# Attention over a graph mask, one core: half of the first mask pieces written as bytes by ScalarE and stored from SyncE, and another way through the last tail

## The chip, the cores and the metric

The kernel runs on one core of a Trainium2 chip. The metric is the device time of one execution in microseconds; lower is better. The median of three runs of the kernel before is 3595.21 us (3592.2 to 3596.22). One execution was profiled; the page and every time below come from it.

In the profile PE is TensorE (PEld its weight loads), DVE is VectorE, ACT is ScalarE, POOL is GpSimd and SP is SyncE. SP computes nothing here: it is the queue from which most plain transfers are issued. POOL issues transfers too, among them all that add to what is already in memory.

## The reference

For each of eight frames there are 2048 rows of 256 channels. One layer is computed, and then a residual and a norm. `adj` is one 2048 x 2048 mask for all frames and heads.

```python
def layer(x, adj, ...):                       # x: (8, 2048, 256), H = 8 heads of D = 32
    q, k, v = split(x @ w_qkv)                # each (F, N, H, D)
    scores = einsum('fnhd,fmhd->fhnm', q, k) / sqrt(D)
    scores = where(adj > 0, scores, -1e9)
    t = einsum('fhnm,fmhd->fnhd', softmax(scores), v)
    x = layernorm(x + t, ln1_g, ln1_b)
    f_out = relu(x @ w1 + b1) @ w2 + b2
    return layernorm(x + f_out, ln2_g, ln2_b)
out = layernorm(x + layer(x, adj, ...))       # the last norm has no scale or shift
```

## The kernel before

**Items.** The attention is cut into 1024 items (f, qc, g, mb): frame, one of four chunks of 512 queries, one of two groups of four heads, one of sixteen blocks of 128 keys. `scores` (L202) makes four 128x512 score tiles on PE; DVE adds the mask to two at a time (L213), which also moves them out of PSUM; ACT takes the exponential of all four (L217); `values` (L221) multiplies by V and adds up in one PSUM bank over the sixteen blocks.

**Sums of the exponentials.** The denominators need the sum over the sixteen blocks. `add_up` (L242) folds the tiles: blocks 0, 3, 6, 8, 11, 13 and 15 by additions on POOL (L249), two chains of four by accumulating transfers from POOL's queue (L246), block 14 stays alone. `denominator` (L273) multiplies the four remaining tiles by a matrix of ones on PE (L283), turns the result (L290) and takes reciprocals on DVE (L295).

**The tail of a chunk.** After the second head group, `outcome` (L302) turns the attention output on PE (L313), multiplies it by the reciprocals on DVE (L314) into `y`, and adds the rows of `x` to it with an accumulating transfer from POOL's queue (L317). `tail` (L321) does norm 1, turns the rows (L330), runs the feed-forward layer (L341, L342, L351), adds it to `y` (L353), does norm 2, multiplies by the scale and adds the shift on POOL (L356, L358), adds `x` once more by an accumulating transfer (L360), does norm 3 and stores 512 KB from SP (L363). `norm` (L252) takes statistics of four 256-channel rows on DVE (L256, L257), makes the reciprocal root for all four in four small POOL operations (L260 to L264, the power on L261), and applies it in four ACT instructions (L267).

**Order.** Every engine executes in the order in which the program emits its instructions; there is no reordering by a scheduler. The loop over items (L457) emits the attention. Everything else is a generator in the list `fill`: `start` (L369) adds one with a time and a due item, and `advance` (L375) moves each on by one `yield`. A `yield` of a number waits so many items; `BANK` asks for the one bank that an item may give away; `ROOM` allows two tails at a time. While items run, `bank` (L85) hands out the one PSUM bank that is not collecting the values (`state["side"]`, L87); in the first stretch, where no side is set, it goes round five. After the last item a loop (L483) moves the generators on until they end. Since the order is that of emission, a tail that is cut by many yields lies scattered behind the work of others, and one with few yields lies together.

**The first stretch.** `begin` (L404) loads the mask as sixteen int32 pieces of 512 x 512 (`fetch`, L408, one MB each, from SP). For each piece, a conversion on DVE makes bf16: 0 where there is an edge, -57344 where not (L426). `mask_blocks` (L117) turns it on PE in two halves of eight 128x128 transposes into a PSUM bank each (L124), and DVE writes each half as fp8 (L127); the result goes to the DRAM tile `MD` through POOL's queue (L128, 128 KB a half), from where later chunks reload it. In the first four pieces `begin` also turns the rows of frame 0 (L430), stores them to the DRAM tile `XD` through POOL's queue (L431), and makes keys and values; in the next four keys and values of the second head group (L437). Two score items are computed after the eighth piece (L443). All of these use tiles of the pool `pp` (11 buffers); a fetch is emitted after the conversion of each piece, five pieces ahead.

Of the kernel before, what the change touches and what calls it, by code (L numbers as in the profile page):

```python
# [11 lines left out]
BF16 = mybir.dt.bfloat16  # L12
I32 = mybir.dt.int32
F8 = mybir.dt.float8e5
AF = mybir.ActivationFunctionType
# [3 lines left out]
P = 128  # L19
# [10 lines left out]

MASKED = -57344.0


# [20 lines left out]
def fast_path(ctx, tc, cst, x, adj, out, RS):  # L54
# [62 lines left out]
    def mask_blocks(qc, mc, cv, to=None):  # L117
        for half in range(2):
            yield BANK
            ps = bank(BF16)  # L120
            for r in range(2):
                for j in range(TPC):
                    rr = 2 * half + r
                    nc.tensor.transpose(ps[:, r, j * P:(j + 1) * P], cv[:, j, rr * P:(rr + 1) * P], identb)  # L124
            k = 2 * mc + half
            m = to[half] if to else mask_piece(0, qc, k)
            nc.vector.tensor_tensor(m, ps, cst["ones"][:, 0:1, None].to_broadcast([P, 2, CH]), ALU.min, saturate=False)  # L127
            nc.gpsimd.dma_start(MD[qc, k], words(m))  # L128

# [108 lines left out]
    MOVED = ((1, 4, 7, 10), (2, 5, 9, 12))  # L238
    ALONE = 14
    SUM = 4  # L240

    def add_up(item):  # L242
        f, qc, g, mb = item
        for chain in MOVED:
            if mb in chain[1:]:
                nc.gpsimd.dma_start(PT[f, qc, g, chain[0]], PT.pop(item), accum_op=ALU.add)  # L246
        if mb in POOLED[1:]:
            first = PT[f, qc, g, POOLED[0]]
            nc.gpsimd.tensor_tensor(first, first, PT.pop(item), ALU.add)  # L249
# [23 lines left out]
    def denominator(f, qc, g):  # L273
        grp = (f, qc, g)
        terms = [PT.pop((f, qc, g, ALONE))] + [PT.pop((f, qc, g, chain[0])) for chain in MOVED + (POOLED,)]
        yield BANK
        ps = bank()
        for n, term in enumerate(terms):
            if n == 2:
                yield BANK  # L280
            for h in range(4):
                r = D * h
                nc.tensor.matmul(ps[r:r + D, :], cst["ones"], term[:, h, :], start=(n == 0), stop=(n == 3))  # L283
        dT = op.tile([P, CH], F32, name="dT")
# [13 lines left out]
        if g == 1:  # L298
            begin = items.index((f, qc, g, LAST)) + SUM + 2
            start(begin, outcome(f, qc), begin)  # L300

    def outcome(f, qc):  # L302
        yield ROOM
        state["tails"] += 1
        rc = RC.pop((f, qc))
        xin = x[f, qc * CH:(qc + 1) * CH, :].rearrange("(p j) c -> p j c", p=P)
        y = yp.tile([P, TPC, C], F32, name="y")
        for gg in range(2):
            oT = OT.pop((f, qc, gg))
            yield BANK  # L310
            ps = bank()
            for j in range(TPC):
                nc.tensor.transpose(ps[:, j * P:(j + 1) * P], oT[:, j::TPC], ident)  # L313
            nc.vector.tensor_tensor(y[:, :, gg * P:(gg + 1) * P].rearrange("p j (h d) -> p j h d", d=D),  # L314
                                    ps.rearrange("p (j h d) -> p j h d", h=4, d=D),
                                    rc[:, :, 4 * gg:4 * gg + 4, None].to_broadcast([P, TPC, 4, D]), ALU.mult)
        nc.gpsimd.dma_start(y, xin, accum_op=ALU.add)  # L317
        begin = items.index((f, qc, 1, LAST)) + SUM + 2
        start(begin + 10, tail(f, qc, y, xin), begin + 26)

    def tail(f, qc, y, xin):  # L321
        yield from norm(y)
        yield TURNED
        state["turned"] = True
# [21 lines left out]
        for jj in range(0, TPC, 2):  # L346
# [6 lines left out]
            nc.vector.tensor_tensor(z[:, jj:jj + 2, :], ps.rearrange("p (b c) -> p b c", c=C), z[:, jj:jj + 2, :], ALU.add)  # L353
        yield 1
        yield from norm(z)
        nc.gpsimd.tensor_tensor(z, z, rows(cst["g2r"]), ALU.mult)  # L356
        yield 1
        nc.gpsimd.tensor_tensor(z, z, rows(cst["be2r"]), ALU.add)  # L358
        yield 1
        nc.gpsimd.dma_start(z, xin, accum_op=ALU.add)  # L360
        yield 7
        yield from norm(z)
        nc.sync.dma_start(out[f, qc * CH:(qc + 1) * CH, :].rearrange("(p j) c -> p j c", p=P), z)  # L363
        state["tails"] -= 1

# [38 lines left out]
    def begin():  # L404
# [16 lines left out]
        while cols:  # L421
# [3 lines left out]
            cv = two[:, c % 2 * TPC * CH:(c % 2 + 1) * TPC * CH].rearrange("p (j m) -> p j m", m=CH)  # L425
            nc.vector.tensor_scalar(cv, col, 0.0, MASKED, op0=ALU.is_le, op1=ALU.mult)  # L426
            fetch()
            xT = rows[c][:, 2:4, :]
            if qc == 0:
                yield from turn_rows(rows[c][:, 0:2, :].rearrange("p a (b c) -> p (a b) c", c=C), xT)  # L430
                nc.gpsimd.dma_start(XD[0][c], xT)  # L431
                XT[0, c] = xT
# [24 lines left out]
    for t, (f, qc, g, mb) in enumerate(items):  # L457
# [4 lines left out]
        if f + 1 < F:  # L462
            for what, *which in NEXT.get((2 * qc + g, mb), []):
                due = t + MB // 2 if what is turn else items.index((f + 1, 0, which[1], which[0] * TPC)) - LEAD - 1
                start(t, what(f + 1, *which), due)
        if mb:
            advance(t, 1)
# [12 lines left out]
        if mb == LAST:  # L480
            start(t + SUM, denominator(f, qc, g), t)
    t = len(items)
    while fill:  # L483
        t += 1
# [237 lines left out]
```

## Time and profile before

| | before |
|---|---|
| median of the runs | 3595.21 us |
| the profiled execution | 3592.91 us |
| its span, first to last instruction | 3590.9 us |
| PE busy | 3199.5 us (89%) |
| DVE busy | 2745.6 us (76%) |
| ACT busy | 2413.7 us (67%) |
| POOL busy | 2628.5 us (73%) |
| mean granted TensorE clock | 0.986 |
| first mask conversion starts | 16.20 us |
| last mask eviction ends | 99.89 us |
| last addition of exponentials on POOL ends | 3524.02 us |
| last activation starts (of four) | 3582.07 us |

In a row of the time line the first number is the start in us from the span's start, the second the duration; then the engine, the line of the kernel, the operation, what it writes and reads with shapes, and how many instructions were merged. In brackets stands how long the engine had been idle before and what ended that. A row of the busy time by stretch gives the stretch, its length, the busy time and instructions of each engine, the granted TensorE clock (1.00 is full), the mean share of the DMA engines and the rate in GB/s.

### The profile page before, as it was taken

The numbers are of one execution on the slowest core, as the hardware profiler recorded it, in microseconds if no ns is written. First come the engines' busy times: TensorE is split into PE (matmuls) and PEld (weight loads), VectorE is DVE, ScalarE is ACT, GpSimd is POOL, SyncE is SP. The second block draws the span as 40 slices with busy tenths as digits, with TensorE's granted clock in tenths as the row PEclk, the third lists the DMA queues.
The fourth block names the chain that finished last, engine by engine and source line by source line (L and its number), as shares of the span: only waits on it lengthen the run. The fifth ranks groups of instructions, "written<-read, shape, count | busy, mean of one in ns | idle before, by whom it ended". The sixth has DMA issues, their size and how long they took to land. (4 is left out here: it accounts for less than half of the span.)

```text
span 3590.9 us, 54434 instructions
## 1 busy us (share of the span) xinstructions
PE 3199.5 (89%) x22020; PEld 1036.2 (29%) x22020; DVE 2745.6 (76%) x3191; ACT 2413.7 (67%) x1921; POOL 2628.5 (73%) x1399
## 2 busy tenths in 40 slices
PE   6889998899988999998989999999998999988884
PEld 4222332223322233222322223222232223322221
DVE  5788768886788867877778776887768877688882
ACT  2576667776677766777677676677667776677772
POOL 3577768787688766878677776787767877688885
PEclk8999999999999999999999999999999999999997
DMA  8677768778578767778667778677776778587763
GB/s 300 138 157 159 171 149 179 153 152 187 130 158 188 154 155 154 155 165 186 156 143 163 158 159 183 131 165 172 156 178 144 151 163 176 137 170 161 152 143 73
DMA packets 146226, 576.52 MB, mean 161 GB/s; under 512 B 14608, under 2 KB 63248, under 8 KB 96816
## 3 DMA queue, kind: packets, MB, share of 16 engines
q0 software_dynamic: 66960, 443.19, 61.0%
q1 hardware_dynamic: 78192, 128.48, 10.5%
q8 instruction: 174, 2.85, 0.3%
q10 hardware_dynamic: 816, 1.31, 0.1%
q14 instruction: 84, 0.69, 0.1%
HBM read 132.52 MB, written 37.75 MB: 47 GB/s over the span
## 5 line engine op out<-in xcount | busy, mean ns | idle before, releaser
L213 DVE TENSOR_TENSOR p<-s,mask 128x1024 f32<-128x1024 f32 x2048 | 2410.2, 1219 | 697.8 <-PE s L210 409.0
L217 ACT ACTIVATE p<-p 128x2048 f32<-128x2048 f32 x1024 | 1957.4, 1911 | 1059.0 <-DVE p L213 820.4
L249 POOL TENSOR_TENSOR p<-p 128x2048 f32<-128x2048 f32 x384 | 1858.4, 4888 | 423.6 <-ACT p L217 421.6
L210 PE MATMUL s<-qT,kT 32*128 32x512 f32 x8192 | 1171.0, 641 | 169.3 <-DVE p L213 165.1
L229 PE MATMUL x<-p,v 128*32 128x512 f32 x8192 | 1092.9, 606 | 0.0
L246 POOL DMA_DIRECT2D p<-p x384 | 385.3, 1022 | 362.3 <-ACT p L217 149.9
L210 PEld LDWEIGHTS s<-qT,kT 32*128 32x128 f32 x8192 | 320.3, 183 | 797.9 <-DVE p L213 648.5
L229 PEld LDWEIGHTS x<-p,v 128*32 128x32 f32 x8192 | 161.3, 108 | 778.5 <-issue 544.1
L267 ACT ACTIVATE y<-y,nb,rs 128x256 f32<-128x256 f32 x384 | 224.9, 589 | 37.8 <-POOL nb L264 37.8
L283 PE MATMUL x<-p,ones 128*32 128x512 f32 x2048 | 243.9, 594 | 2.7 <-POOL p L249 1.2
L167 PE MATMUL x<-in,wqkv 128*128 128x512 f32 x472 | 234.0, 618 | 13.8 <-ACT turned L331 7.8
L256 DVE BATCH_NORM_STATS2 st<-y 128x6 f32<-128x256 f32 x384 | 160.0, 417 | 24.9 <-DMA y<-in_x_dram 24.9
L341 PE MATMUL x<-turned,w1s 128*128 128x512 f32 x256 | 130.6, 633 | 21.3 <-ACT hT L342 20.4
L167 PEld LDWEIGHTS x<-in,wqkv 128*128 128x128 f32 x472 | 79.9, 189 | 174.2 <-issue 71.7
L351 PE MATMUL x<-w2s,hT 128*128 128x256 f32 x512 | 127.6, 392 | 2.6 <-ACT hT L342 1.8
L192 PE MATMUL x<-wqkv,in 128*128 128x128 f32 x896 | 114.9, 281 | 7.2 <-ACT kT L169 7.0
L192 PEld LDWEIGHTS x<-wqkv,in 128*128 128x128 f32 x896 | 104.2, 191 | 55.9 <-ACT kT L169 38.3
L351 PEld LDWEIGHTS x<-w2s,hT 128*128 128x128 f32 x512 | 92.0, 189 | 66.6 <-ACT hT L342 29.4
L283 PEld LDWEIGHTS x<-p,ones 128*32 128x32 f32 x2048 | 63.4, 110 | 163.7 <-issue 124.4
L261 POOL TENSOR_TENSOR rs<-rs,mhalf 128x4 f32<-128x4 f32 x96 | 99.5, 1036 | 8.0
L330 PE MATMUL x<-ident,y 128*128 128x128 f32 x256 | 47.7, 297 | 53.2 <-ACT turned L331 37.7
L358 POOL TENSOR_TENSOR y<-y,be2r 128x1024 f32<-128x1024 f32 x32 | 94.2, 2943 | 0.2
(89 smaller groups left out, 1401.0 us busy)
## 6 DMA issues: line engine op xcount, KB each, us to landing
p<-p POOLq DMA_DIRECT2D x384, 1024.0 KB, 9.8
y<-in_x_dram POOLq DMA_DIRECT2D x64, 512.0 KB, 6.2
mask<-md SPq DMA_DIRECT2D x248, 128.0 KB, 5.7
in<-xd SPq DMA_DIRECT2D x59, 512.0 KB, 7.3
p<-in_adj_dram SPq DMA_DIRECT2D x16, 1024.0 KB, 15.4
out_dram<-y SPq DMA_DIRECT2D x32, 512.0 KB, 4.7
in<-in_x_dram SPq DMA_DIRECT2D x28, 512.0 KB, 5.6
xd<-in SPq DMA_DIRECT2D x28, 512.0 KB, 8.9
```

Source lines behind the costliest of these rows:

```text
L167: nc.tensor.matmul(ps, wqkv[:, a, k0:k0 + P], xT[:, a, :], start=(a == 0), stop=(a == 1))
L192: nc.tensor.matmul(ps[:, j * P:(j + 1) * P], xT[:, a, j * P:(j + 1) * P], wqkv[:, a, 2 * C + g * P:2 * C + (g + 1) * P], start=(a == 0), s ...
L210: nc.tensor.matmul(ps2[half][:, j, :], KT[f, mb // TPC, g][r:r + D, (mb % TPC) * P:(mb % TPC + 1) * P], QT[f, qc, g][r:r + D, :], start=Tr ...
L213: nc.vector.tensor_tensor(pt[:, 2 * half:2 * half + 2, :], ps, MK[f, qc, mb // 2][:, mb % 2, None, :].to_broadcast([P, 2, CH]), ALU.add)
L217: nc.scalar.activation(PT[item], PT[item], AF.Exp, scale=1.0 / math.sqrt(D))
L229: nc.tensor.matmul(O[grp][r:r + D, :], V[f, mb // TPC, g][:, mb % TPC, r:r + D], PT[item][:, h, :], start=(mb == 0), stop=(mb == LAST))
L246: nc.gpsimd.dma_start(PT[f, qc, g, chain[0]], PT.pop(item), accum_op=ALU.add)
L249: nc.gpsimd.tensor_tensor(first, first, PT.pop(item), ALU.add)
L256: nc.vector.bn_stats(st, t[:, j, :])
L267: nc.scalar.activation(t[:, j, :], t[:, j, :], AF.Identity, bias=nb[:, j:j + 1], scale=rs[:, j:j + 1])
L283: nc.tensor.matmul(ps[r:r + D, :], cst["ones"], term[:, h, :], start=(n == 0), stop=(n == 3))
L351: nc.tensor.matmul(ps[:, (j - jj) * C:(j - jj + 1) * C], hT[:, d, j * P:(j + 1) * P], w2s[:, d, :], start=(d == 0), stop=(d == 1))
```

## The change

In the first stretch the conversion is made in two halves by key columns. The first half is written with -5 and the second with -57344 as before. The first half's turned bank is written by ScalarE as signed bytes (the byte of -5 is the bit pattern of -57344 in this fp8 format, and 0 stays 0); the second by VectorE as before. The stores to `MD`, and those of frame 0 to `XD`, go through SP's queue. 

For the last group of the last chunk, blocks 13 and 15 are not added on POOL but become terms of their own in the denominator. The last chunk's tail is a function of its own, `finish`, emitted in one go: the rows of `x` are loaded eight items before the end and added on DVE; the norms work in halves of two rows; scale, shift and residual are four half operations on DVE; the store is in two halves. After the last item, `bank` goes round five banks again. The division (`divide`) and the feed-forward layer (`feed_forward`) become functions that the old and the new tail share.

```diff
 def mask_blocks(qc, mc, cv, to=None):
...
-            nc.vector.tensor_tensor(m, ps, cst["ones"][:, 0:1, None].to_broadcast([P, 2, CH]), ALU.min, saturate=False)
-            nc.gpsimd.dma_start(MD[qc, k], words(m))
+            if half:
+                nc.vector.tensor_tensor(m, ps, cst["ones"][:, 0:1, None].to_broadcast([P, 2, CH]), ALU.min, saturate=False)
+            else:
+                nc.scalar.copy(m.bitcast(I8), ps)
+            nc.sync.dma_start(MD[qc, k], words(m))
...
+    ENDED = (13, 15)
...
-        if mb in POOLED[1:]:
+        if mb in POOLED[1:] and not ((f, qc, g) == items[-1][:3] and mb in ENDED):
...
+        if (f, qc, g) == items[-1][:3]:
+            terms[3:3] = [PT.pop((f, qc, g, b)) for b in ENDED]
...
-            start(begin, outcome(f, qc), begin)
+            start(begin, outcome(f, qc) if (f, qc) != (F - 1, NCK - 1) else finish(f, qc), begin)
...
+    def norm_halves(t):
+        both = []
+        for h in range(0, TPC, 2):
+            mv = small.tile([P, 2, nc.vector.BN_AGGR_DIM], F32, name="mv")
+            for j in range(2):
+                st = small.tile([P, nc.vector.BN_STATS_DIM], F32, name="st")
+                nc.vector.bn_stats(st, t[:, h + j, :])
+                nc.vector.bn_aggr(mv[:, j, :], st)
+            rs = small.tile([P, 2], F32, name="rs")
+            nc.gpsimd.tensor_scalar(rs, mv[:, :, 1], EPS, 1.0, op0=ALU.add, op1=ALU.mult)
+            nc.gpsimd.tensor_tensor(rs, rs, cst["mhalf"][:, 0:2], ALU.pow)
+            nb = small.tile([P, 2], F32, name="nb")
+            nc.vector.scalar_tensor_tensor(nb, mv[:, :, 0], -1.0, rs, op0=ALU.mult, op1=ALU.mult)
+            both.append((h, rs, nb))
+        for h, rs, nb in both:
+            for j in range(2):
+                nc.scalar.activation(t[:, h + j, :], t[:, h + j, :], AF.Identity, bias=nb[:, j:j + 1], scale=rs[:, j:j + 1])
+
+    def finish(f, qc):
+        y = yp.tile([P, TPC, C], F32, name="y")
+        xr, xb = state["rows"], take([P, TPC, C], F32)
+        yield from divide(f, qc, y)
+        nc.vector.tensor_tensor(y, y, xr, ALU.add)
+        norm_halves(y)
+        nc.vector.tensor_tensor(xb, xr, rows(cst["be2r"]), ALU.add)
+        yield from feed_forward(y)
+        z = y
+        norm_halves(z)
+        for h in range(0, TPC, 2):
+            nc.vector.tensor_tensor(z[:, h:h + 2], z[:, h:h + 2], rows(cst["g2r"])[:, h:h + 2], ALU.mult)
+            nc.vector.tensor_tensor(z[:, h:h + 2], z[:, h:h + 2], xb[:, h:h + 2], ALU.add)
+        norm_halves(z)
+        dst = out[f, qc * CH:(qc + 1) * CH, :].rearrange("(p j) c -> p j c", p=P)
+        for h in range(0, TPC, 2):
+            nc.sync.dma_start(dst[:, h:h + 2], z[:, h:h + 2])
...
-            nc.vector.tensor_scalar(cv, col, 0.0, MASKED, op0=ALU.is_le, op1=ALU.mult)
+            for half, what in enumerate((CODE, MASKED)):
+                part = slice(half * 2 * P, (half + 1) * 2 * P)
+                nc.vector.tensor_scalar(cv[:, :, part], col[:, :, part], 0.0, what, op0=ALU.is_le, op1=ALU.mult)
...
-                nc.gpsimd.dma_start(XD[0][c], xT)
+                nc.sync.dma_start(XD[0][c], xT)
...
+        if t == len(items) - MB // 2:
+            state["rows"] = take([P, TPC, C], F32)
+            nc.sync.dma_start(state["rows"], x[f, qc * CH:(qc + 1) * CH, :].rearrange("(p j) c -> p j c", p=P))
...
     t = len(items)
+    state["side"] = None
     while fill:
```

## The prediction

> **What bounds the kernel now.** I read the slices of the page first, then the busy time by stretch, then the time lines of both ends. The change touches only the two ends, so those matter, not the totals.
>
> ```profile
> PEclk8999999999999999999999999999999999999997
> ...
> 62.00:100.00 38.00, 15.17 (x132) 13.07 (x132) 28.85 (x25) 1.91 (x1) 11.04 (x15) 0.50 0.37 136
> 100.00:3500.00 3400.00, 3098.22 (x21376) 972.80 (x21376) 2660.53 (x3076) 2367.32 (x1855) 2549.35 (x1306) 1.00 0.73 159
> 3500.00:3591.00 91.00, 37.85 (x176) 15.72 (x172) 24.07 (x63) 26.27 (x38) 47.17 (x40) 0.72 0.34 75
> ```
>
> The columns of the last three lines are the stretch, its length, the busy time of PE, PEld, DVE, ACT and POOL, PE's granted clock, the DMA share and GB/s. The middle 3400 us run PE at full clock; their instructions and order stay as they were, so I let them shift as a block. From 62 to 100 us no engine is full and PE runs at half clock: this is a chain. ACT has 1.91 us of work there.
>
> *The first stretch* handles 16 adjacency pieces (I call them columns). Columns 8 to 15, from VectorE's time line and then TensorE's:
>
> ```profile
> 62.85 1.22 DVE L426 TENSOR_SCALAR p<-p 128x2048 bf16<-128x2048 int32 x1
> 65.20 1.23 DVE L127 TENSOR_TENSOR in<-s,ones 128x1024 fp8e5<-128x1024 bf16 x1 [1.13 <-PE s L124]
> 66.34 1.22 DVE L127 TENSOR_TENSOR in<-x,ones 128x1024 fp8e5<-128x1024 bf16 x1
> 67.47 1.22 DVE L426 TENSOR_SCALAR p<-p 128x2048 bf16<-128x2048 int32 x1
> ...
> 64.12 1.04 PE L124 MATMUL s<-identb,p 128*128 128x128 bf16 x8 [3.60 <-DVE p L426]
> 64.95 1.06 PE L124 MATMUL x<-identb,p 128*128 128x128 bf16 x8
> ```
>
> One column is 67.47 - 62.85 = 4.62 us: a conversion on DVE, the first eight transposes, then two evictions one behind the other, and PE waits until the next conversion. Columns 0 to 7 are different: PE also makes keys and values there and is busy 4.3 to 5.0 of every 5 us from 10 to 55 us, period 5.8 and then 4.45 us; DVE does not set it.
>
> *The last tail*, from the time line of all engines:
>
> ```profile
> 3524.07 1.06 PE L283 MATMUL x<-p,ones 128*32 128x512 f32 x8 [1.16 <-POOL p L249]
> 3536.37 0.43 DVE L256 BATCH_NORM_STATS2 st<-y 128x6 f32<-128x256 f32 x1 [6.13 <-DMA y<-in_x_dram]
> 3538.97 1.03 POOL L261 TENSOR_TENSOR rs<-rs,mhalf 128x4 f32<-128x4 f32 x1
> 3546.05 3.78 PE L341 MATMUL x<-turned,w1s 128*128 128x512 f32 x4 [0.87 <-ACT turned L331]
> 3550.61 3.78 PE L341 MATMUL x<-turned,w1s 128*128 128x512 f32 x4 [0.78 <-ACT hT L342]
> 3558.04 1.59 PEld L351 LDWEIGHTS x<-w2s,hT 128*128 128x128 f32 x8 [1.28 <-DVE y L353]
> 3567.10 2.34 POOL L356 TENSOR_TENSOR y<-y,g2r 128x1024 f32<-128x1024 f32 x1 [2.19 <-ACT y L267]
> 3569.52 2.34 POOL L358 TENSOR_TENSOR y<-y,be2r 128x1024 f32<-128x1024 f32 x1
> 3577.84 0.43 DVE L256 BATCH_NORM_STATS2 st<-y 128x6 f32<-128x256 f32 x1 [14.87 <-DMA y<-in_x_dram]
> 3582.07 2.07 ACT L267 ACTIVATE y<-y,nb,rs 128x256 f32<-128x256 f32 x4 [15.05 <-POOL nb L264]
> ```
>
> Everything here is one serial chain: two residual loads stand on it (6.1 and, with the two POOL passes, 13 us), and PE waits for its single free PSUM bank. The last activation ends at 3584.14, the span 6.76 later.
>
> **The first stretch, part by part.** The conversion becomes two of 1024 elements; the first half's transposes wait for the first alone. That half is evicted by ACT, the other by DVE.
>
> A half conversion has no row. From one 1.22 us row for 2048 it is 0.61 if all of it scales. The Trainium skill (VectorE: DVE Perf Modes, the section on the TRN2 errata) speaks against this: each VectorE instruction carries a fixed term, about 150 cycles as measured there, or 0.156 us at 0.96 GHz. Then a half is (1.22 - 0.16)/2 + 0.16 = 0.69. The row of 1.22 agrees with 1067 ns of elements plus that term, so I take 0.69; the second half begins 0.09 before the first ends, as evictions do (1.23 long, 1.14 apart), and ends at 1.29. Now one column, at half clock: first transposes start at 0.73, issue for 0.83 (64.95 - 64.12), the second eight follow at 1.56, end at 2.62; DVE evicts from 2.66; the next conversion starts 1.14 later. Period **3.80** (3.72 by plain scaling), against 4.62. Eight columns: 8 x 0.82 = **6.6 us**. ACT's eviction, estimated at 1.07 from two 512-element copies in 1.07, hides in its idle time; without that cover (it runs from 1.60 to 2.67, DVE's own from 2.66 to 3.80) up to its whole 1.07 a column would show.
>
> Bounds: if a half conversion costs as much as a whole, the period is 4.6 and nothing is gained; if PE's clock rises to full, transposes shrink to 0.45 an eight and the period is near 3.05, 12.5 us gained. PE's share only goes from 41% (1.89 of 4.62) to 50%, and the clock fell in 55 to 60 us with PE at 46%, so I stay with half clock.
>
> Around it: column 3's conversion waits 2.10 us for its load, and PE 0.44 for that; the stores of XD, now behind the loads in one queue, no longer overtake it: -0.4. The two score pairs after column 7 wait for its second eviction (56.29); with one DVE eviction it ends near 55.6: -0.7. In columns 1 to 3 ACT's eviction stands ahead of the turning copies: 0.1 each, +0.3. Sum of the stretch: 6.6 + 0.4 + 0.7 - 0.3 = **7.4 us**.
>
> *SP's queue.* It takes 36 transfers from POOL (32 pieces, 4 of XD), each behind an ACT or DVE result, and the later adjacency loads queue behind them. [...] The load issued after column c is for column c+6. Walking through the queue at 410 GB/s (the DMA rate from 20 to 60 us), column 7's load lands near 41 us and is converted near 51; column 15's near 76, converted near 88. No wait, at least 8 us of cover. POOL loses only issue work, and there it was idle (busy 11.0 of 38).
>
> **The tail, part by part**, in times of before:
>
> 1. Sums. Pieces 13 and 15 leave POOL's chain and go to PE as two more terms, 8 instructions or 0.87 us each (24 take 2.78). The first term no longer waits for the residual add of the tail before: it starts near 3519.15. Third term: its accumulating DMA lands near 3520.6 (issue 3511.31 + 9.3). The last term starts at 3519.15 + 5 x 0.87 = 3523.5, not 3524.07: **-0.6** only. What POOL gives up, PE takes over.
> 2. Free banks let both turns of the attention output run together: second division ends 3528.15 instead of 3530.18, so another **-1.5**.
> 3. The load (6.13 us of waiting) becomes a DVE add of 1024 elements, 1.22 by the 128x1024 rows, plus 0.3 of small flag operations around it: statistics start near 3529.65 instead of 3536.37, **-6.7** with 1 and 2. The preload is issued long before.
> 4. Normalisation in halves. DVE is in order, and the small product of half 0 waits for POOL ahead of half 1's statistics, so the halves follow one another: 2 x (1.07 statistics + 0.09 + 0.27 + power + 0.07 + 0.12). The power on 128x2 has no row; between the fixed 0.2 of other small POOL operations and 1.03 for 128x4 I take 0.62. Half: 2.23; both 4.46, then two activations 1.1: 5.55 against 6.29, **-0.7**; with power at 1.03, +0.1.
> 5. Feed-forward. Two banks remove the waits 0.87, 0.78 and 0.87. The clock: by the profile PE went from 3546.05 to about 3554.3 before it was full, with two gaps of 0.8. The Trainium skill (TensorE: Matmul & The Clock Gate, Part 1) has it rise after one busy free-running window of 3.4 us, so 3.4 to 6.8 us without gaps. By the row's 8.2 us both layers stay slow (7.6 us); by the rule they gain 1.3. The new run has no gaps, so I take the rule. Second residual add ends near 3548.05 instead of 3560.83: **-12.8** in all. POOL's two passes of this tail and two of the tail before (4 x 2.4) just fit below it.
> 6. Scale, shift and residual: four half passes of about 0.63 on DVE in place of 4.8 on POOL and 5.9 of load. Statistics of the last norm start near 3555.0, not 3577.84: **-22.8**.
> 7. The end. The last activation would come near 3560.6. But the *tail before* is advanced in small steps while this one is written at once: its last statistics stand behind this tail's on DVE, its reciprocal roots on POOL, activations on ACT and its 512 KB store on SP too. After 3559.5: 2.17 statistics, 1.95 + 0.1 on POOL, 2.07 activations: 3565.8. It ends the kernel, with a whole store: 6.76 as before. So the tail gives 3584.14 - 3565.8 = **18.3 us**, not 23.
>
> **Sum**: 7.4 + 18.3 = 25.7. Span 3590.9 - 25.7 = 3565.2; the profiled execution took 3592.91, 2.0 more than its span, so 3567.2. It was 2.3 below the median of the runs shown, 3595.21: **3569.5**.
>
> **Rivals.** *The first stretch keeps its pace* (half conversions dear, or ACT's eviction late): gain 0.8 there, 3576. For it: only one conversion size in the trace. Against: PE's order lets the first half go. *PE's clock rises* in columns 8 to 15: 5.9 more, 3563.6; against it the 46% above. *Slower*: SP's ordered queue starves the conversions. A load takes 15.4 us (median) with six outstanding; with fewer than three, between stores, 12 columns would come at load pace. They would need (25.7 + 7.2)/12 more than planned, near 6.8 us each, to end above 3602; six loads in 15.4 are 2.6 each, and fewer outstanding land sooner (6.3 at least), so it needs a stall that the page does not show. *The change does nothing*: the middle would have to give back 26 us.
>
> **Numbers.** Forecast 0.66 (own range 3565 to 3574: power, clock, runs), same pace 0.15, clock 0.10, slower 0.05, nothing 0.04. The range 3562 to 3577 takes in the first three. 0.2% (7 us) is about what a measurement here tells from no change: faster 0.92, within 0.03, slower 0.05.
>
> **What would show it.** Right: conversion to conversion 3.8 us at clock 0.5; no load on the last chain; the last store that of the tail before. Wrong: conversions waiting for loads, a half conversion near 1.2, a middle longer than 3400.

## The result, and the profile after

| | before | after |
|---|---|---|
| median of the runs | 3594.69 us | 3565.82 us (3564.28 to 3567.47) |
| the profiled execution | 3592.91 us | 3567.08 us |
| its span | 3590.9 us | 3565.3 us |
| last mask eviction ends | 99.89 us | 94.18 us |
| last exponential starts | 3511.33 us | 3507.38 us |
| last activation ends | 3584.14 us | 3561.34 us |
| from there to the end of the span | 6.76 us | 3.96 us |

The changed kernel takes 0.992 of the time before, 95% interval 0.9903 to 0.9938: 28.9 us less. The forecast was 3569.5.

The busy time by stretch of the changed kernel (stretch, length, PE, PEld, DVE, ACT, POOL, clock of PE, DMA share, GB/s):

```profile
63.40:94.20 30.80, 15.11 (x128) 13.00 (x128) 19.56 (x25) 9.91 (x9) 0.00 (x0) 0.50 0.43 134
94.20:3475.00 3380.80, 3082.90 (x21248) 968.71 (x21252) 2642.76 (x3052) 2353.54 (x1842) 2530.50 (x1294) 1.00 0.73 160
```

Columns 8 to 15 now last 30.7 us (63.46 to 94.18) instead of 37.0 (62.85 to 99.89), ACT works in them, POOL does nothing, and PE still has half its clock. The time line of one such column in the changed kernel:

```profile
67.27 1.28 DVE L482 TENSOR_SCALAR p<-p 128x1024 bf16<-128x1024 int32 x2
68.01 1.03 PE L126 MATMUL x<-identb,p 128*128 128x128 bf16 x8 [1.92 <-DVE p L482]
68.83 1.06 PE L126 MATMUL s<-identb,p 128*128 128x128 bf16 x8
69.08 1.01 ACT L132 CAST in<-x 128x1024 int8<-128x1024 bf16 x1 [2.69 <-PE x L126]
69.93 1.23 DVE L130 TENSOR_TENSOR in<-s,ones 128x1024 fp8e5<-128x1024 bf16 x1 [1.38 <-PE s L126]
71.08 1.29 DVE L482 TENSOR_SCALAR p<-p 128x1024 bf16<-128x1024 int32 x2
```

PE starts 0.74 us into the pair of half conversions (one alone takes 682 to 695 ns in this trace), ACT evicts the first half beside PE's second, and DVE waits 1.38 for PE before its own eviction. 71.08 - 67.27 = 3.81 us; the columns alternate between 3.81 and 3.86. The first scores after column 7, in the kernel before and in the changed one (column 7's conversion starts at 51.76 and at 51.90):

```profile
56.34 1.14 PE L210 MATMUL s<-qT,kT 32*128 32x512 f32 x8 [2.00 <-DVE in L127]
...
56.49 1.14 PE L215 MATMUL s<-qT,kT 32*128 32x512 f32 x8 [1.32 <-DVE in L130]
```

The last tail of the changed kernel, from the time line of all engines:

```profile
3515.26 5.36 PE L292 MATMUL x<-p,ones 128*32 128x512 f32 x48
...
3524.01 1.22 DVE L372 TENSOR_TENSOR y<-y,in 128x1024 f32<-128x1024 f32 x1
3525.27 0.42 DVE L356 BATCH_NORM_STATS2 st<-y 128x6 f32<-128x256 f32 x1
...
3526.80 0.71 POOL L360 TENSOR_TENSOR rs<-rs,mhalf 128x2 f32<-128x2 f32 x1
...
3532.57 5.50 PE L405 MATMUL s<-turned,w1s 128*128 128x512 f32 x8
...
3542.37 0.69 DVE L417 TENSOR_TENSOR y<-x,y 128x512 f32<-128x512 f32 x1 [0.97 <-PE x L415]
...
3547.67 0.69 DVE L379 TENSOR_TENSOR y<-y,g2r 128x512 f32<-128x512 f32 x1
...
3555.00 0.42 DVE L263 BATCH_NORM_STATS2 st<-y 128x6 f32<-128x256 f32 x1
...
3559.26 2.08 ACT L274 ACTIVATE y<-y,nb,rs 128x256 f32<-128x256 f32 x4 [2.99 <-POOL nb L271]
...
3561.37 0.33 SPq L346 DMA_DIRECT2D out_dram<-y  x1
```

No load stands in this chain any more. Its last three rows are the tail before (L263, L274, L346): its statistics start after the last small product of this tail, and its store is the last.

Between the two ends both kernels do the same work. From the last mask eviction to the last exponential took 3411.44 us before and 3413.20 after in these two executions.

### The profile page after: what moved, and what is told of

Same layout as the page of the kernel before. It is cut to its first block, busy times and chain, and to the rows that moved or that the text cites. A ratio compares the mean times of both kernels' runs of the same rounds, so it can differ in the third digit from the quotient of the medians.

```text
span 3565.3 us, 54466 instructions
## 1 busy us (share of the span) xinstructions
PE 3201.1 (90%) x22036; PEld 1037.4 (29%) x22036; DVE 2734.1 (77%) x3203; ACT 2431.1 (68%) x1937; POOL 2587.3 (73%) x1357
## 5 line engine op out<-in xcount | busy, mean ns | idle before, releaser
L274 ACT ACTIVATE y<-y,nb,rs 128x256 f32<-128x256 f32 x372 | 219.4, 591 | 3.0 <-POOL nb L271 3.0
L263 DVE BATCH_NORM_STATS2 st<-y 128x6 f32<-128x256 f32 x372 | 155.5, 418 | 0.0
L405 PE MATMUL x<-turned,w1s 128*128 128x512 f32 x248 | 123.0, 618 | 19.3 <-ACT hT L406 19.1
L399 POOL TENSOR_TENSOR y<-y,be1b2r 128x1024 f32<-128x1024 f32 x32 | 91.3, 2852 | 0.1
```

The lines of the kernel that those rows point to most:

```text
L263: nc.vector.bn_stats(st, t[:, j, :])
L274: nc.scalar.activation(t[:, j, :], t[:, j, :], AF.Identity, bias=nb[:, j:j + 1], scale=rs[:, j:j + 1])
```

## The experiments

The kernel before ran beside each group: 3596.88 us median with the first four kernels, 3597.71 with the second four, 3598.12 with the last four. Differences below are against those medians, or from stages of the profiled executions. "The stretch" runs from the second conversion to the last mask eviction (the first conversion began anywhere from 16 to 20 us, with the arrival of the first piece, in all kernels); "the middle" from there to the last exponential's start; "the tail" from there to the last activation's end; "the closing" from there to the end of the span.

### The first stretch alone

```diff
-    ENDED = (13, 15)
+    ENDED = ()
...
-            start(begin, outcome(f, qc) if (f, qc) != (F - 1, NCK - 1) else finish(f, qc), begin)
+            start(begin, outcome(f, qc), begin)
...
-        if t == len(items) - MB // 2:
-            state["rows"] = take([P, TPC, C], F32)
...
-    state["side"] = None
```

> The first stretch as changed, the tail as before. By my sum the last mask eviction ends 7.4 us earlier than before and all of it reaches the end: about 3587 where before takes 3594.7. By the trace of the changed kernel it ends only 5.7 earlier, and if the middle is really 1.8 longer because the stretch ends in another way (the loads of the first minutes of the middle, the order of the stores), then only 3.9 arrives: about 3591. If the middle's 1.8 is only scatter between executions, 5.7 arrives: 3589. The closing after the last activation should stay near 6.8, as the tail is that of before.

3587.51 us, 9.4 less than before; ratio 0.9975 (0.9966 to 0.9985). My sum had 7.4 less. The stretch is 71.31 us long against 79.38, and the closing is 4.10 although the tail is that of before; I had expected 6.8. These two make 10.7 us, of which the middle of this execution, 3413.65, takes 2.2 back.

### The tail alone

```diff
-            if half:
-                nc.vector.tensor_tensor(m, ps, ...)
-            else:
-                nc.scalar.copy(m.bitcast(I8), ps)
-            nc.sync.dma_start(MD[qc, k], words(m))
+            nc.vector.tensor_tensor(m, ps, ...)
+            nc.gpsimd.dma_start(MD[qc, k], words(m))
...
-            for half, what in enumerate((CODE, MASKED)):
...
+            nc.vector.tensor_scalar(cv, col, 0.0, MASKED, op0=ALU.is_le, op1=ALU.mult)
...
-                nc.sync.dma_start(XD[0][c], xT)
+                nc.gpsimd.dma_start(XD[0][c], xT)
```

> The tail as changed, the first stretch as before. By my sum 18.3 us less than before: about 3576.4. By the trace of the changed kernel 21.7 (the chain itself 18.8, and 2.8 from a shorter closing after the last activation): about 3573. Theory A: the closing is short because in the new tail POOL's last work lies well before the end, so the closing here is about 4.0. Theory B: it is short because POOL issues 36 transfers fewer in the first stretch; then the closing here is near 6.8 again. The middle should be that of before within 0.5 us if its 1.8 came with the first stretch.

3579.91 us, 17.0 less than before; ratio 0.9949 (0.9935 to 0.9962). My sum had 18.3 less. The tail is 54.15 us against 72.81, and the closing is 6.65. So the shorter closing does not come with the new tail; theory A falls. It comes with the first stretch. The middle is 3413.81, longer than that of before by more than the 1.8 in question, although this kernel has the stretch of before.

### As changed, with the stores on POOL's queue

```diff
-            nc.sync.dma_start(MD[qc, k], words(m))
+            nc.gpsimd.dma_start(MD[qc, k], words(m))
...
-                nc.sync.dma_start(XD[0][c], xT)
+                nc.gpsimd.dma_start(XD[0][c], xT)
```

> As changed, but the mask pieces and the turned rows are stored through POOL's queue again. My prediction gave the move of the stores 0.4 us (the wait of column 3 for its load) and nothing else, so 0.4 slower than the changed kernel, within scatter. Theory B of the closing (fewer transfers issued by POOL make it short) says the closing goes from 4.0 back to 6.8, so 2.8 to 3.2 slower; theory A (POOL's last work lies earlier) says it stays 4.0.

3570.72 us, 26.2 less than before; ratio 0.9926 (0.9911 to 0.9941). The closing is 6.69 again. The instructions of POOL at the kernel's end, in the order before, after, first stretch alone, tail alone, stores on POOL (lowest, median and highest duration in ns, then first and last start in us):

```profile
L689 POOLq INC_SWDGE_SEM  x1: 1386/1386/1386, 3583.7 to 3583.7; - x1
L718 POOLq DRAIN  x3: 46/107/4927, 3585.1 to 3590.6; - x3
```

```profile
L749 POOLq INC_SWDGE_SEM  x1: 799/799/799, 3560.6 to 3560.6; - x1
L778 POOLq DRAIN  x3: 46/107/2518, 3561.4 to 3565.0; - x3
```

```profile
L745 POOLq INC_SWDGE_SEM  x1: 819/819/819, 3579.7 to 3579.7; - x1
L774 POOLq DRAIN  x3: 46/107/2682, 3580.5 to 3584.2; - x3
```

```profile
L773 POOLq DRAIN  x3: 46/254/4764, 3571.8 to 3577.5; - x3
```

```profile
L778 POOLq DRAIN  x3: 46/255/4764, 3562.5 to 3568.3; - x3
```

The longest drain is 4.9 us before and 2.5 after. In the kernel before it begins at 3585.1 and so ends at about 3590.0, later than the last store lands (issued at 3584.2, 2.9 us to landing): POOL's drain ended the span. After the change the drain ends at about 3563.9 and the store lands at about 3564.4, so the store ends it. The drain is 4.76 us with the 36 stores on POOL in both kernels that have the new tail, and 2.52 in each of the kernels that have it without them; with the old tail, which issues two residual loads more from POOL, it is 0.16 longer in both cases. This is theory B. The stretch is 72.89 us. One column in it waited 0.56 us for its mask piece, but with the stores on SP's queue the same stretch took 71.06 to 73.65 us in seven executions, so no cost of POOL's queue shows there. By the stages the move of the stores is worth 2.7 us, all of it in the closing, and not 0.4 in the stretch. By the medians it is some 3 (26.2 against 28.9 and, below, 29.5).

### As changed, with both evictions on VectorE

```diff
-            if half:
-                nc.vector.tensor_tensor(m, ps, ...)
-            else:
-                nc.scalar.copy(m.bitcast(I8), ps)
+            nc.vector.tensor_tensor(m, ps, ...)
...
-            for half, what in enumerate((CODE, MASKED)):
+            for half, what in enumerate((MASKED, MASKED)):
```

> The conversion in halves and the stores through the synchronous queue as changed, but VectorE evicts both halves. This tells the split apart from ScalarE's part. From my durations a column of 8 to 15 is: two half conversions 1.29, first eviction waits for the first eight transposes (end near 1.56 + 0.2), second for the second eight (2.66), then 1.14 + to the next conversion: about 3.8 to 4.05 if the two evictions follow each other and the second ends later by up to 0.25. If ScalarE's share is what makes the gain (rival), the period is back near 4.6. In all 0 to 2 us slower than the changed kernel by the first, 6 by the rival.

3571.87 us, 25.0 less than before; ratio 0.9929 (0.9913 to 0.9944). One column in its time line:

```profile
72.54 1.29 DVE L479 TENSOR_SCALAR p<-p 128x1024 bf16<-128x1024 int32 x2
73.28 1.89 PE L126 MATMUL s<-identb,p 128*128 128x128 bf16 x16 [2.20 <-DVE p L479]
74.36 2.36 DVE L129 TENSOR_TENSOR in<-s,ones 128x1024 fp8e5<-128x1024 bf16 x2 [0.53 <-PE s L126]
76.63 1.28 DVE L479 TENSOR_SCALAR p<-p 128x1024 bf16<-128x1024 int32 x2
```

The period is 4.09 us. So of the 0.78 that a column became shorter (4.62 to 3.84 on the mean), 0.53 is the split: PE starts half a conversion earlier. ScalarE's part is 0.25, because DVE's first eviction lay in the time in which it would have waited for PE's second half anyway.

### As changed, with more transposes

```diff
+        if qc > 1:
+            ps = bank(BF16)
+            for n in range(16):
+                nc.tensor.transpose(ps[:, n // 8, n % 4 * P:(n % 4 + 1) * P], identb, identb)
```

> As changed, with sixteen more transposes of the identity on PE behind each of columns 8 to 15, whose result nobody reads: added work, to fill PE. At half clock they issue in 1.66 us, so PE is busy about 3.5 of each column's 3.85 instead of 1.89. If the clock follows PE's busy share (my clock rival), it rises to full within some 5 to 10 us, transposes take half, and the columns after that come every 3.05 to 3.2: the last mask eviction 3 to 6 us earlier although work was added. If the clock does not rise, the period stays 3.85 (the added transposes lie in PE's wait) and the end is the same within 0.5 us.

3562.92 us; ratio to before 0.9908 (0.9893 to 0.9923). The changed kernel took 3568.67 beside it: 5.8 less with more work, though single runs of the two overlap (3560.56 to 3570.58 against 3565.6 to 3572.33). The busy time by stretch and the time line:

```profile
67.80:87.00 19.20, 13.34 (x197) 11.27 (x195) 14.61 (x20) 6.07 (x6) 0.00 (x0) 0.96 0.55 193
```

```profile
66.39 1.91 PE L137 MATMUL x<-identb 128*128 128x128 bf16 x16
...
68.51 1.36 PE L126 MATMUL s<-identb,p 128*128 128x128 bf16 x16 [0.21 <-DVE p L486]
...
74.25 1.29 DVE L486 TENSOR_SCALAR p<-p 128x1024 bf16<-128x1024 int32 x2
74.99 1.22 PE L126 MATMUL s<-identb,p 128*128 128x128 bf16 x16 [1.08 <-DVE p L486]
76.05 1.06 PE L137 MATMUL x<-identb 128*128 128x128 bf16 x16
77.39 1.28 DVE L486 TENSOR_SCALAR p<-p 128x1024 bf16<-128x1024 int32 x2
```

Sixteen transposes took 1.91 us at 66.39 and 1.06 in each later column: the clock rose at about 69 us, some 4 us after PE became busy almost without a gap (64.71), and stayed up with PE busy 70% of the time. The period is 3.14 to 3.20, near the 3.05 of my clock rival, and the stretch 67.83 us against 71.06 of the changed kernel in the same group. So the rival's price was right, and what kept it away is that PE idles half of each column, 1.92 us at a time. Here its gaps were shorter too (1.02 to 1.08 us); whether the busy share or the length of a gap decides, this run does not separate.

### As changed, with both evictions on ScalarE

```diff
-            if half:
-                nc.vector.tensor_tensor(m, ps, ...)
-            else:
-                nc.scalar.copy(m.bitcast(I8), ps)
+            nc.scalar.copy(m.bitcast(I8), ps)
...
-            for half, what in enumerate((CODE, MASKED)):
-                part = slice(half * 2 * P, (half + 1) * 2 * P)
-                nc.vector.tensor_scalar(cv[:, :, part], col[:, :, part], 0.0, what, op0=ALU.is_le, op1=ALU.mult)
+            nc.vector.tensor_scalar(cv, col, 0.0, CODE, op0=ALU.is_le, op1=ALU.mult)
```

> As changed, but ScalarE evicts both halves as bytes (-5 in both), and the conversion is one instruction again; VectorE does nothing but convert in the first stretch. What bounds a column of 8 to 15 then? ScalarE: two evictions of 1.01 each, 2.0 us. PE: sixteen transposes issue in 1.66 at half clock. Loads: one MB each, 2.6 at 410 GB/s, and with the stores about 2.9 to 3.3. So between 2.0 (ScalarE) and 3.3 (loads) instead of 3.85, 8 columns x 0.6 to 1.8 = 5 to 14 us less than the changed kernel, part of it lost again if columns 0 to 7 get slower by ScalarE's added second eviction (0.3 to 1.0 each in columns 0 to 3). Rival: the chain of a column stays serial, conversion 1.22 + 0.2 + transposes 1.89 + 0.2 + eviction 1.0, since the tile of a pair of columns is shared: then 3.6 to 4.5 and no gain.

3562.24 us, 35.5 less than before; ratio 0.9897 (0.9881 to 0.9914). The stretch is 63.65 us, 7.7 shorter than the 71.31 of the first stretch alone. From DVE's waits and its time line, and then from that of SP's queue:

```profile
DVE p L477 <- DMA p<-in_adj_dram: 6.0, 2, 3.9
```

```profile
69.21 6.89 DVE L477 TENSOR_SCALAR p<-p 128x2048 bf16<-128x2048 int32 x6
...
79.98 1.23 DVE L477 TENSOR_SCALAR p<-p 128x2048 bf16<-128x2048 int32 x1 [3.88 <-DMA p<-in_adj_dram]
...
83.32 1.23 DVE L477 TENSOR_SCALAR p<-p 128x2048 bf16<-128x2048 int32 x1 [2.11 <-DMA p<-in_adj_dram]
...
72.59 1.23 SPq L130 DMA_DIRECT2D md<-in  x2
73.93 0.38 SPq L462 DMA_DIRECT2D p<-in_adj_dram  x1
74.81 0.85 SPq L130 DMA_DIRECT2D md<-in  x2
75.76 0.80 SPq L462 DMA_DIRECT2D p<-in_adj_dram  x1
```

DVE converts six columns one behind the other; ACT and PE follow, PE at a rising clock, and the last two columns wait for loads. The serial rival falls. The conversion's engine and the eviction's engine no longer take turns, and DVE runs ahead until it meets the loads: the cover of 8 us, by which I had excluded waits for loads, was that of slower columns. The last two loads were issued late, each behind a pair of stores in SP's queue that had waited for ACT's evictions (up to 9.3 us for one). So the mechanism of my rival "slower", a queue in order that holds the loads back, does appear here; how much of the two waits it makes was not tried.

### As changed, with the sums on POOL

```diff
-    ENDED = (13, 15)
+    ENDED = ()
```

> As changed, but blocks 13 and 15 of the last group are added on POOL again. My step 1 gave this part 0.6 us, so the second division and all behind it come 0.6 later, measured from the last exponential. Rival: the whole of two POOL additions (2 x 4.9) was saved, then 5 to 9 later. Zero is possible if the denominators still start behind something else.

3570.76 us, 27.0 less than before; ratio 0.9925 (0.9908 to 0.9941). The second division ends 17.24 us after the last exponential's start instead of 16.57 in the changed kernel: 0.67 later, near the 0.6 of step 1.

### As changed, with one bank after the last item

```diff
-    state["side"] = None
```

> As changed, but after the last item one bank is handed out as before instead of five. By my steps 2 and 5: the second turn waits (1.5), the feed-forward pieces wait 0.87 + 0.78 + 0.87, and the clock rises later (1.3 to 2), in all 4.5 to 5.5 us later at the second residual add, measured from the last exponential; the kernel's end moves by the same or by 1 us less, since the tail before ends it. Rival: the clock does not depend on the gaps, then 4.0 and no matmul of the feed-forward faster.

3577.49 us, 20.2 less than before; ratio 0.9941 (0.9925 to 0.9958). The tail is 61.01 us, 7.1 longer than the 53.96 of the changed kernel: 2.6 up to the first statistics and 4.5 up to the second residual add. With one bank the denominators start 0.92 later, the turn of the attention output takes 1.7 more, and the waits in the feed-forward layer are 0.87, 0.87, 0.84, 0.78 and 0.88. So the banks are worth more than I gave them: of the feed-forward layer's waits I had counted three, and there are five (4.24 us in all, not 2.5). In this execution the clock has little part in it. From the time lines of this kernel, and of the first one, whose tail is that of before:

```profile
3541.60 3.72 PE L405 MATMUL x<-turned,w1s 128*128 128x512 f32 x4 [0.87 <-ACT turned L395]
3546.16 1.98 PE L405 MATMUL x<-turned,w1s 128*128 128x512 f32 x4 [0.84 <-ACT hT L406]
```

```profile
3544.38 3.60 PE L405 MATMUL x<-turned,w1s 128*128 128x512 f32 x4 [0.87 <-ACT turned L395]
3548.76 1.98 PE L405 MATMUL x<-turned,w1s 128*128 128x512 f32 x4 [0.78 <-ACT hT L406]
```

With the gaps the two groups take 5.70 and 5.58 us together, and without them eight instructions took 4.50 to 5.91 in the eleven other executions, 5.33 on the mean (5.50 in the changed kernel). The two slow groups of before, 3.78 and 3.78, were one draw of three with gaps; whether gaps make such a draw more likely, three do not tell.

### As changed, with the statistics of both halves first

```diff
-    def norm_halves(t):
+    def norm_halves(t, between=None):
...
+            both.append((h, rs, nb, mv))
+        if between:
+            between()
+        for h, rs, nb, mv in both:
             nc.vector.scalar_tensor_tensor(nb, mv[:, :, 0], -1.0, rs, op0=ALU.mult, op1=ALU.mult)
-            both.append((h, rs, nb))
-        for h, rs, nb in both:
```

> As changed, but the norms in halves make the statistics of both halves before the first half's small product, so that POOL's root of half 0 runs beside the statistics of half 1. By my step 4 the halves follow one another because the small product waits on VectorE for POOL ahead of the other half's statistics; if that is so, each norm is 1.1 to 1.3 us shorter, and the statistics of the tail before come 3.3 to 3.9 earlier. Rival: the wait is elsewhere (POOL's power of the two halves in series), then 0.3 or less per norm.

3566.41 us, 31.3 less than before; ratio 0.9913 (0.9896 to 0.9929). The tail is 49.76 us, 4.2 shorter. From the time line of its first norm:

```profile
3529.69 0.71 POOL L360 TENSOR_TENSOR rs<-rs,mhalf 128x2 f32<-128x2 f32 x1
3529.77 0.39 DVE L356 BATCH_NORM_STATS2 st<-y 128x6 f32<-128x256 f32 x1
...
3530.67 2.10 ACT L368 ACTIVATE y<-y,nb,rs 128x256 f32<-128x256 f32 x4 [6.50 <-DVE nb L366]
```

The power of half 0 runs beside the statistics of half 1. The norm takes 4.60 us from its first statistics to its last activation instead of 5.91: 1.3, three times. This is what step 4 said of the order on VectorE. In the whole time the 4.2 us do not show: 31.3 less is near the 28.9 and 29.5 of the changed kernel, single runs range from 3562.39 to 3569.73, and the middle of the profiled one, 3415.86, is 2.7 longer than in the changed kernel.

### As changed, with the last norm of the tail before brought forward

```diff
+        if (f, qc) == (F - 1, NCK - 2):
+            state["rest"] = z, xin
+            return
...
+        nc.gpsimd.tensor_tensor(z0, z0, rows(cst["g2r"]), ALU.mult)
+        nc.gpsimd.tensor_tensor(z0, z0, rows(cst["be2r"]), ALU.add)
+        nc.gpsimd.dma_start(z0, xin0, accum_op=ALU.add)
         yield from feed_forward(y)
...
-        norm_halves(z)
+        norm_halves(z, between)
...
+        nc.sync.dma_start(out[f, (qc - 1) * CH:qc * CH, :].rearrange("(p j) c -> p j c", p=P), z0)
```

> As changed, but the last norm and the store of the tail before are brought forward: its scale, shift and residual load follow on POOL right after this tail's first norm, its statistics fill VectorE's waits in this tail's second norm, and its 512 KB store goes ahead. By my step 7 the tail before ends the kernel 5 us after this tail would alone (3565.8 against 3560.6), so the last activation comes 4 to 5 us earlier from the last exponential and 3 to 5 us reach the end. Rival: the residual load of the tail before (6 us and more) now arrives in the middle of this tail's norm and holds VectorE up, or POOL's closing after its last work (4.5 us) sets the end; then 0 to 2 us, or a loss.

3566.03 us, 32.1 less than before, and 2.6 less than the changed kernel beside it, whose single runs overlap with these; ratio to before 0.9913 (0.9897 to 0.9928). The tail is 50.09 us, 3.9 shorter than the 53.92 of the changed kernel in the same group: this tail now ends the kernel, as step 7 had it.

### Three together

This kernel has both evictions on ScalarE, the statistics first, and the last norm of the tail before brought forward, with its statistics after those of both halves.

> The three together: ScalarE evicts both halves, statistics first, the last norm of the tail before brought forward. Of the changed kernel, e5_scalar_both gained about 7 to 9 us by the stages, e8_stats_first 4.2 in the tail; with the last norm of the tail before out of the way, another 2 to 4. Sum 13 to 17 less than the changed kernel, 3550 to 3556; the rival is that POOL's closing or the loads take it back, then no better than e5_scalar_both alone (3562).

3553.76 us (3552.83 to 3557.2), 44.4 less than before; ratio 0.9878 (0.9862 to 0.9893). The changed kernel beside it took 3568.67 (3565.6 to 3572.33), so this version is 14.9 faster than that, and beats both. The stretch is 63.42 us. The tail is 49.26, only 0.5 better than with the statistics first alone, so the last two gains do not add up. From the time line of its first norm:

```profile
3519.50 2.35 POOL L379 TENSOR_TENSOR y<-y,g2r 128x1024 f32<-128x1024 f32 x1
3519.57 2.29 DVE L366 SCALAR_TENSOR_TENSOR nb<-mv,rs 128x2 f32<-128x2 f32 x1 [0.90 <-POOL rs L360]
```

A small product that takes 0.16 us elsewhere took 2.29 beside the scale pass of the tail before on POOL, and ended with it. That is 2.1 us on the path. In the second norm the statistics of the tail before (2.1 us) stand ahead of the small products. These two could account for it; I did not separate them.

### The changed kernel again

> The changed kernel itself, on the same chip as the other three: the measure for them. By the earlier runs 26 to 29 us less than before, tail (last exponential to last activation) 53 to 54.5, closing 4.0, the first stretch 75 to 78 from the first conversion. A middle anywhere from 3411 to 3417 would say that its 1.8 us more in the first profile was scatter.

3568.67 us, 29.5 less than before; ratio 0.9917 (0.9904 to 0.9931). The tail is 53.92, the closing 3.95, the middle 3413.10. The stretch is 71.06 us, in the first profile 73.12. Of these 2.06 us, 0.95 lie in the two score items after column 7, and 0.85 between the second conversion and the third (4.94 us against 5.79), where I know no cause. The second conversion and the second group of scores in this execution, and that group in the first profile of the same kernel:

```profile
22.67 1.30 DVE L482 TENSOR_SCALAR p<-p 128x1024 bf16<-128x1024 int32 x2 [0.69 <-DMA p<-in_adj_dram]
...
59.79 1.14 PE L215 MATMUL s<-qT,kT 32*128 32x512 f32 x8 [1.40 <-DVE p L218]
```

```profile
59.03 2.09 PE L215 MATMUL s<-qT,kT 32*128 32x512 f32 x8 [1.40 <-DVE p L218]
```

The clock falls in about this place, before the group in some executions and after it in others: 0.95 us, of one kernel.

## Why the prediction was right

The seven executions with this stretch (changed twice, first stretch alone, sums, bank, statistics, norm forward) have 72.15 us on the mean from the second conversion to the last eviction (71.06 to 73.65); the two with the stretch of before (before, tail alone) have 79.38 and 79.17. That is 7.1 us. Seven tails as changed average 53.97, the two of before 72.81 and 72.24: 18.6. The closing gives 2.8. Together 28.5, against 28.9 and 29.5 by the medians. My sum was 7.4 + 18.3 = 25.7. It also meets the 25.6 between the two profiled spans, but that is partly an accident: there the stretch gave 5.7 and the middle took 1.8, and the closing made up for it.

- **Half conversions at 0.69.** Right: the 32 of the first profile take 682 to 695 ns each, a pair 1.28 to 1.30 us (1.29). Plain scaling would have made 0.61. The rule on the fixed term (VectorE: DVE Perf Modes, the section on the TRN2 errata, in the Trainium skill) chose the right one.
- **Period 3.80, clock half.** Right: 3.81 to 3.86 at 0.50. I argued from PE's share of 46% where the clock fell. The run with more transposes agrees: PE kept the clock with a share of about 70%, and did not get it with 50%; the length of its gaps (1.02 to 1.08 us against 1.92) would explain this as well. ACT's eviction took 1.01 instead of 1.07 and hid.
- **Around the columns: -0.4, -0.7, +0.3.** Near in sum, by luck. From column 1's conversion to column 8's it is 42.34 and 42.14 us with the old stretch and 41.51 on the mean of the seven: 0.7 less, but the seven range from 40.60 to 42.94. Of the parts only the +0.3 shows (columns 2 and 3 take 5.85 us each, 5.75 and 5.71 in the kernel with the tail alone). The -0.7 did not come: the first scores start 4.59 us after column 7's conversion (56.49 - 51.90), before 4.58 (56.34 - 51.76). VectorE's single eviction waits 2.02 us for PE there, which I had left out. And the wait of column 3 for its load, 2.10 in the profile of before, is not there in the kernel with the tail alone, which has the same stretch.
- **SP's queue: no wait.** Right in the first profile; in the second one conversion, the second, waited 0.69 us. The load issued after column c is that of column c+5, not c+6 as I had it. With both evictions on ScalarE two conversions of columns 8 to 15 waited more (3.88 and 2.11).
- **Stores moved off POOL: only 0.4 (in "column 3's conversion waits").** Wrong in size and in place. With the stores on POOL the closing was 2.7 longer, and the stretch no longer than its scatter. "POOL loses only issue work, and there it was idle" left out what POOL does at the end.
- **Tail, steps 1 to 3.** Step 1 is right to 0.1 (0.67). The first statistics come at 3529.22 in times of before (3.95 added), predicted 3529.65. Without the free banks they would come 2.6 later, and step 2 had counted 1.5 for these; the missing piece is the denominators' wait for a bank, 0.92, which I had put into step 1.
- **Step 4, norms at 5.55.** 5.91: the power on 128x2 takes 0.71 and not 0.62, which makes half of the difference. Three norms make 1.1. The order that I gave as the reason is shown by the run with the statistics first.
- **Step 5, the feed-forward layer.** Its sum came out (3547.01 against 3548.05), a term of it did not. The 1.3 us for a clock that rises earlier without gaps are not shown to be an effect of the change: with gaps two of three executions were as fast (5.58 and 5.70 against 5.50), and 7.56 was the third. The rule of the Trainium skill (TensorE: Matmul & The Clock Gate, Part 1) agrees with the run with more transposes, where the clock rose about 4 us after PE became busy, but in the tail the eight instructions vary by 1.4 us from one execution to the next without any gap (4.50 to 5.91). What I missed were two more waits for a bank.
- **Steps 6 and 7.** Right: the first statistics of this tail's last norm at 3554.28 in times of before (3555.0), the last activation at 3565.29 (3565.8), and it is that of the tail before. The run with its norm brought forward gives 3.9 back, where I had put about 5.
- **"6.76 as before".** This step failed: 3.96. It is most of the 3.7 us by which the forecast missed the median (another 0.5 is the median of before itself, 3594.69 in the later comparison). The run of the tail alone and the one with the stores on POOL show that the closing follows the stores.
- **The middle as a block.** The middle of the kernels with POOL's stores is 3411.44, 3413.81 and 3411.92, of those without 3410.48 to 3415.86 (3419.85 with both evictions on ScalarE, but 3411.55 in the last combination, which has the same stretch). The differences come in jumps, most of about 1 us and of both signs (one of 5.5 in the 3419.85), near the change from one frame to the next, in kernels with the same middle. The changed kernel has nearly the same middle in both of its profiles (3413.20 and 3413.10), but the tail alone, with the stretch of before, has 3413.81. So the 1.8 us need no cause in the change; what makes the jumps is open.

Of the rivals, none came: the pace rose, the clock stayed half, and in the changed kernel no conversion after the second waited for a load. The total is nearer than some of its parts, since terms that I had wrong (the -0.7, the 1.3 for the clock) and terms that I had missed (two waits for a bank, the closing) went opposite ways.

## What to carry to other kernels

A chain of two engines that take turns gained here when the pieces got smaller (0.53 us a column) and again when turns were given to another engine; look then at what the freed time uncovers (here loads that stood behind stores in one queue). A transfer's queue can cost something at the end of the kernel too, 2.7 us here: read what the queue's engine does after its last useful instruction, and whether it or the last store ends the span. Before a difference of two profiled executions is explained, look at a second execution of the same kernel, since here the start, the clock and the middle each moved by 1 to 4 us by themselves.

## What I had not expected of the hardware

- GpSimd's drain at the end took 4.76 us where 36 stores more had gone through its queue, and 2.52 where not; the difference, 2.25 us, is 62 ns for each on the mean. The semaphore increment ahead of it took 1.35 and 0.80. With 490 transfers from POOL in all and 454, the drain isn't simply proportional to their number; what sets it is open.
- More work on PE made the first stretch faster: with sixteen idle transposes per column the clock was 0.96 instead of 0.50, and a column became 0.66 us shorter.
- ScalarE's eviction of 128x1024 bf16 into bytes takes 1.01 us, VectorE's into fp8 1.23.
- A VectorE product of 128x2 took 2.29 us beside a GpSimd pass of 2.35 instead of 0.16, and ended with it (3521.86 and 3521.85).
